# A four-layer graph network on one core: layer 0 of the next group starts on another event, sums and `rf` get two buffers, adj is read twice, one bias add and some copies change engine, and the order of work is found anew

## The chip, the cores and the metric

The kernel runs on one core of one Trainium2 chip. The core has a matrix engine (TensorE, in the profile PE, with its weight loads as PEld), a vector engine (VectorE, DVE), a scalar engine for activations and copies (ScalarE, ACT), a general engine (GpSimd, POOL) and a sync engine (SyncE, SP) from whose queue this kernel issues its DMAs. Each engine takes its instructions in the order of its own queue; engines wait for each other through semaphores.

The metric is the time of one execution on the device in microseconds (us). The median of the runs shown stands for a kernel. About 0.3% is what a measurement of this kernel can tell from no change.

## What is computed

There are 128 graphs of 64 nodes, with 128 features a node (x) and a 64x64 weighted adjacency matrix each (adj). About a quarter of adj is nonzero: an undirected edge is drawn from two chances of 0.125, and the diagonal is always set. The weights are between 0.05 and 5. Four layers follow each other, each as x + layer(relu(layernorm(x))). Cut to what matters:

```python
# layer 0: a filter made from each edge's length, summed over neighbours
g  = exp(coeff * (e[..., None] - offsets)**2)      # e is adj, 64 offsets
h  = ssp(g @ W1.T + b1)                            # ssp(x) = softplus(x) - ln 2
Wf = (h @ W2.T + b2) * A                           # A is adj too
rf = r @ Wa.T                                      # r is the normed x
y  = sum_j rf[j] * (Wf * A)[i, j]
y  = ssp(y @ Wd1.T + bd1) @ Wd2.T + bd2

# layer 1: hyperbolic attention
h = proj(mobius_add(proj(mobius_matvec(W, x)), hyp_bias))
x_loc = logmap(h_i, h_j)                           # for every pair i, j
a = silu(concat(x_self, x_loc) @ att_w1.T + att_b1)
support = sum_j sigmoid(a @ att_w2.T + att_b2) * x_loc * adj
out = proj(expmap(mlp(concat(x_self, support)), h)) # then silu in the tangent space

# layer 2: adj with d_norm on both sides, times x, times W, plus b
# layer 3: concat(x, where(deg > 0, adj.T @ (x @ Ws) / max(deg, 1) + x @ Wr, 0)) @ W_upd
```

Layers 0 and 1 have work for every edge and every feature; they are nearly all of the time. Layers 2 and 3 are small products on whole graphs.

## The kernel before

**Groups and slots.** The graphs are taken in 16 groups of 8. A tile of one group is 128 partitions (two graphs of 64 nodes) by four pairs. The edge work is sparse: in each graph the nodes are sorted by degree, and each node gets a fixed number of slots that its place in this order allows. The slots fall in three classes (c = 0, 1, 2): a graph has 512 slots of class 0 (the first 8 neighbours of each node), 512 of class 1 (the next 8) and 264 of class 2 (what is left, for the 48 nodes of highest degree). `oh` (bf16, 1,288 columns a pair) marks the neighbour that is in a slot, and the weights of the edges, spread over the slots, are the tiles `va`.

**Stages.** Each group goes through seven Python generators, called streams here, of `sparse_stack`:

- `load` (L1384) issues the DMAs of adj (L1389) and x (L1390) on SP's queue.
- `order` (L1395) counts degrees, makes the permutation `perm`, sorts x into `xp` and adj into `adjT` by TensorE products, and makes `oh` by comparing each neighbour's position `pos` with the slot numbers `slot_k`. Within it `normed_x` makes layer 0's `rf`, the tile `a2`.
- `layer0` (L1512) makes the sums over neighbours, `ys` (tiles `y0`, `y1`, `y2`, one for each class). In it `weights_of` makes `va`, the slot weights; `squares` makes the coefficients times weights; `duo` and `filter_of` make the edge filter (`e`, then `ex`, through exp and ln); `neighbours` fetches rf of each slot's neighbour through a TensorE product into PSUM (`big`) and copies it to SBUF as `ra`. VectorE multiplies filter by `ra` (`ex<-big,c_L_gnn_b,ra`) and sums over slots (`y<-ex`).
- `layer1_nodes` (L1652) begins with `bd1` and the softplus of layer 0's output and ends with x after layer 0, `x<-sm,xp`, and the nodes' part of layer 1. Many of its steps are small operations on [128, 4].
- `layer1_edges` is the attention over the same slots: geometric coefficients for each slot (`coefs_of`), a Silu on ScalarE, a Tanh, and weighted sums. `rest1` is the node part behind it, `rest2` (L2121) layers 2 and 3 and the output's DMA (L2239).

**Who sets the order.** The class `Weave` builds the program once, on the host. A stream yields wherever it changes engine, with `on(engine, *takes, after=..., table=...)`: the engine of the next piece, buffers that the piece takes, named events it waits for, and the ScalarE table it needs. `Weave` keeps an estimated clock for each engine and each stream (`about` estimates an instruction). `step` picks, among the pieces that could start soonest on one engine, the one of lowest key; the key is the stream's rank (2 x group + the stage's due) plus an offset from the table `LATE`, which lists one number for each piece of a stream by the stream's name. The queues of PE, DVE, ACT and POOL are then fixed in that order. All instructions but the DMAs are issued in one helper line (L853), so in the profile they are told apart by tile names.

Buffers are counted by `w.ring(n, names)`: n pieces may hold a named buffer at a time, and one that finds it taken can't be picked. The lines that matter here:

```python
w.ring(1, "sm", "sl", "two", "ys", "rf", "U", "a0", "a1", "r0", "x2")
w.ring(2, "va2", "ra", "th", "x", "xp", "nodes", "att", "e")
...
w.ring(5, "adj")
```

So before the change one set of `ys` and one `rf` exist: the layer 0 of two groups cannot be open at once. `layer0(g)` says so too:

```python
yield on(DVE, "ys", after=prior(("order", g), ("layer0", g - 1), ("va1", g - 2)) + [("weights0",)])
```

The event ("layer0", g) comes when all sums of group g are made, ("va0", g) already when its slot weights are made, and ("va1", g) when the weights of the attention of g are.

**The tables of ScalarE.** ScalarE needs a table set loaded for exp and ln, and another for Silu and Tanh. The main loop at the end of `sparse_stack` runs an iteration `it` of four phases, silu, log, silu, log, each with the events that must have come before it ends; with these names the last phase takes layer 0 of group it+2 and the nodes of group it+1, and the third the edges of group `it`. A piece that needs the other table can't be picked.

**adj.** It has five buffers: `order` reads it for the sort, and `rest2`, some three groups later, reads the same tile in its last product.

Of the kernel before, what the change touches and what calls it, by code (L numbers as in the profile page):

```python
# [11 lines left out]
F32 = mybir.dt.float32  # L12
U32 = mybir.dt.uint32
I32 = mybir.dt.int32
# [6 lines left out]
NP = 4  # L21
# [763 lines left out]
def about(engine, op, args, kw):  # L785
# [14 lines left out]
    if engine == ACT:  # L800
# [5 lines left out]


LATE = {
    "attention": (0, -0.5),
    "coefs_of": (1.25, 0.75, -2.25),  # L810
    "coefs_of2": (2.75,),
    "duo": (2.5, 3.5),
    "duo2": (0, 2.5, -2),
    "filter_of": (0.75, 3, -0.25, -2.25, -2, -2.75),
    "filter_of2": (-2.75, 1.75, 2.5, 1.75, -2.5),
    "layer1_nodes": (0, -0.25, 0, 0, 0, 0, 0, 3, -3.5, 0, 0, 0, -0.5, -5.5, 0, 2.25, -1.75, 0, 0, 0,
        0, 0, 0, -2.5, 0, 0, 0, 0, 0, -1.25, 0, 0, 0, 2, 0, 0.75, 0, 0, 0, 0, 0, 0, 0, 0, 0.5),
    "neighbours": (-0.25, -3.5),
    "neighbours2": (1.25,),
    "normed_x": (0, 0, 0, 0, 0, 0, 1.5),  # L820
    "one_minus_z": (3.75,),
    "order": (-0.25, -2.75, 2.25, 0, 0, -5, 0, -3.75, 0, 1.75, -6.75, -3, 3.5, 0, 0, -2.75, -2.75,
        3.25, 1.75, 0.5),
    "rest1": (-3, 0, 0, -3, 0, 0, 0, -3.5, -1.75, 0, 0, 0, 0, 0, -1.75, 0, 0, 0, 3.75),
    "rest2": (2.25, 4.5, 0, 0, 0, 0, 0, 0, 0, 0, 0, -4, 0, -3.75, 0, 1.25, 0, 0, 0, 0, -3, 0, -2.25,
        0, -3.5, 0, 0, 1.25, 3),
    "rows": (0, -1.25),
    "rows2": (2.5,),
    "scores_of": (-1.25, -1.5, -3.5, -1.5),
    "scores_of2": (0, -3.25, 0, -3.5),  # L830
    "slots_ranks": (3.5, 0, 4.75),
    "squares": (2.25, 9.5),
    "squares2": (0, 2.75),
    "turned_from": (3.5,),
    "weights_of": (-3,),
    "weights_of2": (0, -2.5, -2.25),
}


# [30 lines left out]
def on(engine, *takes, after=(), table=None):  # L870

    return engine, takes, after, table
# [98 lines left out]
def sparse_stack(ctx: ExitStack, tc: tile.TileContext, ins, out: bass.AP, flag):  # L971
# [65 lines left out]
    V.tensor_scalar(last_d, bm(ident2, NP), last, None, ALU.mult)  # L1037


    slot_k = const.tile([P, SLOTS + SLOTS % 2], BF, name="slot_k")  # L1040
    slot_r = const.tile([P, SLOTS + SLOTS % 2], BF, name="slot_r")
    rooms = [(name, k) for name in ("e2", "e4", "bR", "rt", "rs", "mask", "e1") for k in range(2)]

    def raw_tile():

# [24 lines left out]
    def slots_ranks():  # L1070
        for c, blocks in enumerate(BLOCKS):
            yield on(DVE)
            at = OFFS[c]
            for k, r0, n, k0 in blocks:
                ki = edge.tile([P, 1024], I32, name="ex", tag="ex", bufs=3)
                G.iota(ki[:, 0:k * n].rearrange("q (n k) -> q n k", n=n), [[0, n], [1, k]], base=k0 - 128,
                       channel_multiplier=0)
                V.tensor_copy(slot_k[:, at:at + k * n], ki[:, 0:k * n])
                V.tensor_copy(slot_r[:, at:at + k * n].rearrange("q (n k) -> q n k", n=n),
                              bl(ident2[:, r0:r0 + n], k))  # L1080
                at += k * n

        w.event("slots")
# [120 lines left out]


    HALF = [slice(0, N), slice(N, P)]
    w.ring(1, "sm", "sl", "two", "ys", "rf", "U", "a0", "a1", "r0", "x2")
    w.ring(2, "va2", "ra", "th", "x", "xp", "nodes", "att", "e")
    w.ring(3, "va", "ex", "big", "oh", "x1")
    w.ring(4, "adjT")  # L1210
    w.ring(5, "adj")

    def evac(dst, src):

# [2 lines left out]
    def wtile(name, bufs=None):  # L1217
        return wide.tile([P, NP, D], F32, name=name, tag=name, **({"bufs": bufs} if bufs else {}))
# [35 lines left out]
    def graphs_mm(pt, lhsT, rhs):  # L1254

        for p in range(NP):
            for h in HALF:
                T.matmul(pt[h, p, :], lhsT=lhsT[h, p, :], rhs=rhs[h, p, :], start=True, stop=True)
# [93 lines left out]
    def part(t, at, k, n):  # L1352

        return t[:, :, at:at + k * n].rearrange("q p (n k) -> q p n k", n=n)
# [28 lines left out]

    def load(g, st):  # L1384
        yield on(DVE, "x", "adj")
        x = st["x"] = pers.tile([P, NP, D], F32, name="x", tag="x")
        adj = st["adj"] = pers.tile([P, NP, N], F32, name="adj", tag="adj", bufs=5)
        gs = slice(2 * NP * g, 2 * NP * (g + 1))
        nc.sync.dma_start(out=adj, in_=adj_d[gs].rearrange("(p b) i j -> (b i) p j", b=2))  # L1389
        nc.sync.dma_start(out=x, in_=x_d[gs].rearrange("(p b) i d -> (b i) p d", b=2))  # L1390
        st["x_used"], st["adj_used"] = w.token("x"), w.token("adj")
        w.wait(5)
        w.event("load", g)

    def order(g, st):  # L1395
# [31 lines left out]
        def normed_x():  # L1427
            yield on(DVE, "a0", "rf")
            st["rf_used"] = w.token("rf")
            raw, mv, sr = ttile("o_raw", NP, 6), ttile("o_mv", NP, 2), ttile("sr", bufs=2)  # L1430
            bn(mv, raw, xp)
            st["sr"] = sr
            yield on(POOL)
            G.tensor_scalar(sr, mv[:, :, 1], EPS_LN, None, ALU.add)
            power(sr, sr, -0.25)
            yield on(POOL)
            h = wtile("a0")
            G.tensor_tensor(h, xp, bl(mv[:, :, 0], D), ALU.subtract)
            yield on(POOL, after=[("weights0",)])
            G.tensor_tensor(xp, xp, bm(bd2s, NP), ALU.add)  # L1440
            yield on(PE, "sm", "a1")
            pt = transposes(h)
            w.release("a0")
            yield on(ACT)
            hT = wtile("a1")
            act(hT, pt, AF.Relu)
            w.release("sm")
            yield on(PE, "sm", after=[("wa",)])
            pt = pairs_mm(hT, lambda p: waT)
            w.release("a1")  # L1450
            yield on(ACT)
            st["rf"] = wtile("a2")
            evac(st["rf"], pt)
            w.release("sm")
            w.event("rf", g)
# [2 lines left out]
        yield on(PE, "sm")  # L1458
        pt = bank(N)
        graphs_mm(pt, adj, perm)  # L1460
        yield on(ACT)
        half = etile("o0")
        evac(half, pt[:, 0:NP, :])
# [19 lines left out]
        for c in range(3):  # L1483
            for at, k, r0, n in blocks_of(c):
                yield on(DVE, after=[("slots",)])
                at += OFFS[c]
                ks = slot_k[:, at:at + k * n].rearrange("q (n k) -> q n k", n=n)
                V.tensor_tensor(part(oh, at, k, n), bl(pos[:, :, r0:r0 + n], k),
                                ks.unsqueeze(1).to_broadcast([P, NP, n, k]), ALU.is_equal)
        yield on(DVE, after=[("rf", g)])  # L1490
        w.event("order", g)

# [18 lines left out]

    def layer0(g, st):  # L1512

        yield on(DVE, "ys", after=prior(("order", g), ("layer0", g - 1), ("va1", g - 2)) + [("weights0",)])
        oh, adjT, rf, sr = st["oh"], st["adjT"], st["rf"], st["sr"]
        ys = st["ys"] = [wtile(f"y{c}") for c in range(2)]
        ys.append(wide.tile([P, 2 * NP, RC], F32, name="y2", tag="y2"))
        st["ys_used"] = w.token("ys")
        ras = {}

# [31 lines left out]
        def neighbours(c, p, k, factors):  # L1552

            yield on(PE, "big", "ra", after=[("f", g, c, p)])
            W = WIDTHS[c]
            nb = big()
            for b, rows in enumerate(HALF):
                T.matmul(nb[:, b, 0:W], lhsT=rf[rows, p, :], rhs=factors[0][rows, k, :],
                         start=True, stop=True)
            factors[1]()  # L1560
            w.event("nb", g, c, p)
            yield on(ACT)
            ra = edge.tile([P, 2, 512], F32, name="ra", tag="ra")
            act(ra[:, :, 0:W], nb[:, :, 0:W], AF.Copy)
            w.release("big")
            ras[c, p] = ra, w.token("ra")
            w.event("ra", g, c, p)
# [86 lines left out]
    def layer1_nodes(g, st):  # L1654
# [9 lines left out]
        T.matmul(pre.rearrange("q (x r) -> q x r", r=N)[:, :, 0:RC], lhsT=wd1T, rhs=ys[2],  # L1664
                 start=False, stop=True)
        w.release("ys", st["ys_used"])
        yield on(DVE)
        V.tensor_scalar(flat(spn), pre, bd1, None, ALU.add)
        w.release("sm")
        V.tensor_scalar(ex, spn, SOFT_MAX, None, ALU.min)  # L1670
        w.event("soft_ready", g)
        yield on(ACT, table="log")
# [181 lines left out]
        V.scalar_tensor_tensor(e1, gram, -2.0, h2b, ALU.mult, ALU.add)  # L1854
        V.tensor_tensor(e3, e1, R, ALU.add)
        V.scalar_tensor_tensor(e3, e3, 0.0, e2, ALU.max, ALU.mult)
        rt, rs, mask = etile("rt"), etile("rs"), etile("mask")
        V.tensor_scalar(rt, e3, MIN_NORM2, None, ALU.max)
        yield on(ACT, table="log")
        act(rt, rt, AF.Ln)  # L1860
# [20 lines left out]
        V.scalar_tensor_tensor(rt, e4, -0.5, rt, ALU.mult, ALU.add)  # L1881
        V.tensor_tensor(rt, rt, rs, ALU.mult)
        yield on(DVE)
        series(rt, e3, mask, rs)
        yield on(DVE)
        V.tensor_tensor(rt, rt, e2, ALU.mult)
        qd = dense.tile([P, NP, 2, N], F32, name="qd", tag="qd", bufs=2)
# [232 lines left out]

    def rest2(g, st):  # L2121

        yield on(PE, "sm", after=prior(("rest1", g), ("rest2", g - 1)) + [("weights2",)])
        adj, adjT, x2 = (st[n] for n in ("adj", "adjT", "x2"))
        gs = slice(2 * NP * g, 2 * NP * (g + 1))
        dn = ttile("dn")
        pt = bank()
        for p in range(NP):
# [103 lines left out]
        yield on(PE, "sm")  # L2232
        pt = bank()
        graphs_mm(pt, adj, xs)
        w.release("adj", st["adj_used"])
        yield on(DVE)
        plus_scaled(y, pt, rdeg, y)
        w.release("sm")
# [64 lines left out]
```

## Time and profile before

| what | us |
|---|---|
| runs, median (lowest to highest) | 2124.67 (2119.98 to 2125.86) |
| the profiled execution, its own time | 2121.52 |
| its span, first to last instruction | 2119.6 |
| PE busy (11,223 instructions) | 1806.3 (85%) |
| PEld busy | 866.0 (41%) |
| DVE busy (4,828) | 1847.9 (87%) |
| ACT busy (3,364) | 1641.1 (77%) |
| POOL busy (362) | 364.5 (17%) |
| chain that ended last, by engine | PE 37%, DVE 36%, ACT 19%, issue 7% |
| DMA, all queues | 13.94 MB, 7 GB/s mean |

Busy is the time in which an engine had an instruction at work; several engines are busy at once, so the shares don't add up. The chain is followed back from the last instruction to whatever released each step, and its shares do. DMA is of no weight: the 16 DMA engines are at work for a few per cent of the span. The page's slices show how even the run is between its start and its end:

```profile
PE   4869897998989898998989889898989889896773
PEld 2333343444444344444444444444434444443342
DVE  5669789999999999999999999999999999897742
ACT  3767887979698887979798897969888796975531
```

Each digit is the busy share, in tenths (9 is 90% or more), of one of 40 slices of 53 us. Three of the costlier groups of instructions give a feeling for the sizes:

```profile
L853 PE MATMUL big<-ex,w2T 128*128 128x512 f32 (+1 forms) x768 | 320.2, 542 | 41.8 <-ACT ex L853 20.6
L853 ACT ACTIVATE ra<-big 128x528 f32<-128x528 f32 (+1 forms) x192 | 166.3, 886 | 8.1 <-PE big L853 7.6
L853 DVE SCALAR_TENSOR_TENSOR ex<-big,c_L_gnn_b,ra 128x1024 f32<-128x1024 f32 x128 | 163.7, 1279 | 16.0 <-PE big L853 15.6
```

A row has the line, the engine, the operation, the tile written and those read, the size and the number of instructions; then their busy time in us and the mean of one in ns; then the engine's idle time just before them and what ended most of it.

### The profile page before, as it was taken

The numbers are of one execution on the slowest core, as the hardware profiler recorded it, in microseconds if no ns is written. First come the engines' busy times: TensorE is split into PE (matmuls) and PEld (weight loads), VectorE is DVE, ScalarE is ACT, GpSimd is POOL, SyncE is SP. The second block draws the span as 40 slices with busy tenths as digits, with TensorE's granted clock in tenths as the row PEclk, the third lists the DMA queues.
The fourth block names the chain that finished last, engine by engine and source line by source line (L and its number), as shares of the span: only waits on it lengthen the run. The fifth ranks groups of instructions, "written<-read, shape, count | busy, mean of one in ns | idle before, by whom it ended". The sixth has DMA issues, their size and how long they took to land.

```text
span 2119.6 us, 31941 instructions
## 1 busy us (share of the span) xinstructions
PE 1806.3 (85%) x11223; PEld 866.0 (41%) x11223; DVE 1847.9 (87%) x4828; ACT 1641.1 (77%) x3364; POOL 364.5 (17%) x362
## 2 busy tenths in 40 slices
PE   4869897998989898998989889898989889896773
PEld 2333343444444344444444444444434444443342
DVE  5669789999999999999999999999999999897742
ACT  3767887979698887979798897969888796975531
POOL 1011012021212203021221202121220302111121
PEclk9979999999999999999999999999999999997765
DMA  2000000000000000000000000000000000000000
GB/s 55 3 6 1 1 6 1 6 8 6 1 8 6 8 6 8 6 8 6 1 8 6 9 6 9 6 1 8 6 9 1 9 1 6 1 1 6 6 5 8
DMA packets 29531, 13.94 MB, mean 7 GB/s; under 512 B 10544, under 2 KB 29360, under 8 KB 29360
## 3 DMA queue, kind: packets, MB, share of 16 engines
q1 hardware_dynamic: 29360, 11.80, 2.1%
q8 instruction: 90, 1.47, 0.3%
q14 instruction: 81, 0.66, 0.1%
HBM read 7.61 MB, written 4.19 MB: 6 GB/s over the span
## 4 chain that ended last, share of the span: by engine, by line
PE 37%; DVE 36%; ACT 19%; issue 7%; POOL 0%; SPq 0%; DMA 0%; DVEq 0%; ACTq 0%; POOLq 0%
PE big L853 25%; PE sm L853 9%; ACT ex L853 6%; DVE va L853 5%; DVE ex L853 4%; PE sl L853 4%; ACT e L853 4%; DVE th L853 4%; DVE y L853 2%; ACT ra L853 2%; DVE ah L853 2%; DVE v L853 2%; ACT n L853 2%; DVE att L853 2%; DVE oh L853 1%
## 5 line engine op out<-in xcount | busy, mean ns | idle before, releaser
L853 PE MATMUL big<-ex,w2T 128*128 128x512 f32 (+1 forms) x768 | 320.2, 542 | 41.8 <-ACT ex L853 20.6
L853 ACT ACTIVATE ex<-big,c_L_gnn_att_b 128x1024 f32<-128x1024 f32 (+1 forms) x192 | 185.5, 974 | 105.0 <-PE big L853 103.2
L853 PE MATMUL big<-e,w1T 64*128 64x512 f32 (+1 forms) x768 | 201.5, 624 | 68.0 <-ACT e L853 47.8
L853 ACT ACTIVATE ex<-big,c_L_gnn_b 128x1024 f32<-128x1024 f32 (+1 forms) x192 | 185.7, 976 | 44.1 <-PE big L853 44.0
L853 PEld LDWEIGHTS big<-ex,w2T 128*128 128x128 f32 x768 | 131.7, 189 | 198.6 <-ACT ex L853 69.5
L853 PE MATMUL big<-va,U 64*128 64x512 f32 (+1 forms) x768 | 186.5, 563 | 29.1 <-DVE va L853 26.8
L853 PE MATMUL big<-va,a 64*128 64x512 f32 (+1 forms) x768 | 181.1, 568 | 10.7 <-DVE k_s L853 3.8
L853 PE MATMUL sl<-ex,aw2b 128*64 128x512 f32 (+1 forms) x768 | 180.7, 549 | 5.5 <-ACT th L853 4.3
L853 DVE SCALAR_TENSOR_TENSOR ex<-big,c_L_gnn_b,ra 128x1024 f32<-128x1024 f32 x128 | 163.7, 1279 | 16.0 <-PE big L853 15.6
L853 ACT ACTIVATE ex<-ex 128x1024 f32<-128x1024 f32 (+1 forms) x192 | 173.9, 925 | 0.2
L853 ACT ACTIVATE ra<-big 128x528 f32<-128x528 f32 (+1 forms) x192 | 166.3, 886 | 8.1 <-PE big L853 7.6
L853 DVE TENSOR_REDUCE y<-ex 128x128 f32<-128x1024 f32 x128 | 155.3, 1213 | 0.6
L853 ACT ACTIVATE th<-sl,hab 128x512 f32<-128x512 f32 (+1 forms) x192 | 118.1, 615 | 45.4 <-PE sl L853 45.4
L853 PE MATMUL big<-slot_r,Sx 64*128 64x512 bf16 (+1 forms) x1152 | 138.9, 346 | 0.0
L853 POOL TENSOR_TENSOR k_r<-k_r,exp 128x4 f32<-128x4 f32 x32 | 32.4, 1013 | 583.1 <-DVE k_r L853 578.7
L853 PEld LDWEIGHTS big<-e,w1T 64*128 64x128 f32 x768 | 68.9, 204 | 155.6 <-ACT e L853 55.1
L853 ACT ACTIVATE va<-va,sr 128x512 f32<-128x512 f32 (+1 forms) x192 | 123.1, 650 | 3.1 <-DVE va L853 2.9
L853 PE MATMUL big<-oh,pqs 64*64 64x512 bf16 (+1 forms) x1152 | 123.3, 348 | 0.0
L853 DVE COPY_PREDICATED va<-slot_r,big 128x1024 f32<-128x1024 uint16 (+1 forms) x96 | 106.5, 1111 | 9.7 <-PE big L853 9.7
L853 DVE SCALAR_TENSOR_TENSOR th<-th,oh 128x1024 f32<-128x1024 f32 (+1 forms) x80 | 99.2, 1240 | 13.8 <-ACT th L853 13.8
L853 ACT ACTIVATE e<-e 128x1024 f32<-128x1024 f32 (+2 forms) x144 | 106.7, 752 | 1.1
L853 PE MATMUL big<-va,ones 64*64 64x512 f32 (+1 forms) x768 | 97.4, 559 | 11.0 <-DVE va L853 11.0
(479 smaller groups left out, 3832.4 us busy)
## 6 DMA issues: line engine op xcount, KB each, us to landing
x<-in_x_dram SPq DMA_DIRECT2D x16, 256.0 KB, 2.9
out_dram<-v SPq DMA_DIRECT2D x16, 256.0 KB, 2.3
adj<-in_adj_dram SPq DMA_DIRECT2D x16, 128.0 KB, 2.3
rt<-in_L_gnn_att_w_dram SPq DMA_DIRECT2D x2, 64.0 KB, 1.9
rs<-in_L_gnn_mlp_w_dram SPq DMA_DIRECT2D x2, 64.0 KB, 2.0
wupd<-in_L_gnn_W_upd_dram SPq DMA_DIRECT2D x1, 128.0 KB, 3.6
w<-in_L_gnn_W_msg_dram SPq DMA_DIRECT2D x2, 64.0 KB, 3.3
r_L_gnn_bd<-in_L_gnn_bd_dram SPq DMA_DIRECT2D x1, 64.0 KB, 3.1
```

The lines of the kernel that those rows point to most:

```text
L853: return f(*args, **kw)
```

## The change

1. `layer0(g)` begins after ("va0", g-1), when the group before has its slot weights, in place of ("layer0", g-1), when it has its sums. `ys` and `rf` have two buffers each.
2. `x` and `adj` have one buffer in place of two and five. `order` gives adj back after its product, and `rest2` reads adj again from DRAM, into a tile of its own, `adj2`, with one buffer.
3. `bd1` is added on ScalarE (Identity with a bias), and VectorE's clamp of it is a piece of its own that waits for that.
4. The copy of `ra` from PSUM is on VectorE for groups 0 and 1, and on ScalarE as a plain copy for the others.
5. `slot_k` loses the slots of class 1, whose numbers are those of class 0 plus 8; the comparison for class 1 subtracts the 8 from `pos` in the same instruction. The tile `mask` in `series` is replaced by `e4`, which is free there.
6. The table `LATE` is new, for every stream.

```diff
 LATE = {
-    "attention": (0, -0.5),
-    "coefs_of": (1.25, 0.75, -2.25),
...
+    "attention": (3, 2.5),
+    "coefs_of": (-3.5, -0.25),
...
-    slot_k = const.tile([P, SLOTS + SLOTS % 2], BF, name="slot_k")
+    slot_k = const.tile([P, SLOTS - OFFS[1]], BF, name="slot_k")
...
-    w.ring(1, "sm", "sl", "two", "ys", "rf", "U", "a0", "a1", "r0", "x2")
-    w.ring(2, "va2", "ra", "th", "x", "xp", "nodes", "att", "e")
+    w.ring(1, "sm", "sl", "two", "x", "adj", "adj2", "U", "a0", "a1", "r0", "x2")
+    w.ring(2, "va2", "ra", "th", "ys", "rf", "xp", "nodes", "att", "e")
     w.ring(3, "va", "ex", "big", "oh", "x1")
     w.ring(4, "adjT")
-    w.ring(5, "adj")
...
-            st["rf"] = wtile("a2")
+            st["rf"] = wtile("a2", 2)
...
         graphs_mm(pt, adj, perm)
+        w.release("adj", st["adj_used"])
...
-                V.tensor_tensor(part(oh, at, k, n), bl(pos[:, :, r0:r0 + n], k),
-                                ks.unsqueeze(1).to_broadcast([P, NP, n, k]), ALU.is_equal)
+                if c == 1:
+                    V.scalar_tensor_tensor(part(oh, at, k, n), bl(pos[:, :, r0:r0 + n], k), -8.0, ks,
+                                           ALU.add, ALU.is_equal)
+                else:
+                    V.tensor_tensor(part(oh, at, k, n), bl(pos[:, :, r0:r0 + n], k), ks, ALU.is_equal)
...
-        yield on(DVE, "ys", after=prior(("order", g), ("layer0", g - 1), ("va1", g - 2)) + [("weights0",)])
+        yield on(DVE, "ys", after=prior(("order", g), ("va0", g - 1), ("va1", g - 2)) + [("weights0",)])
...
-            yield on(ACT)
+            first = g < 2
+            yield on(DVE if first else ACT)
             ra = edge.tile([P, 2, 512], F32, name="ra", tag="ra")
-            act(ra[:, :, 0:W], nb[:, :, 0:W], AF.Copy)
+            (V.tensor_copy if first else S.copy)(ra[:, :, 0:W], nb[:, :, 0:W])
...
-        yield on(DVE)
-        V.tensor_scalar(flat(spn), pre, bd1, None, ALU.add)
-        w.release("sm")
+        yield on(ACT)
+        act(flat(spn), pre, AF.Identity, bias=bd1)
+        w.release("sm")
+        yield on(DVE)
         V.tensor_scalar(ex, spn, SOFT_MAX, None, ALU.min)
...
-        yield on(PE, "sm", after=prior(("rest1", g), ("rest2", g - 1)) + [("weights2",)])
-        adj, adjT, x2 = (st[n] for n in ("adj", "adjT", "x2"))
+        yield on(DVE, "adj2", after=prior(("edges", g), ("rest2", g - 1)))
+        adj, adj_used = pers.tile([P, NP, N], F32, name="adj2", tag="adj2", bufs=1), w.token("adj2")
         gs = slice(2 * NP * g, 2 * NP * (g + 1))
+        nc.sync.dma_start(out=adj, in_=adj_d[gs].rearrange("(p b) i j -> (b i) p j", b=2))
+        w.wait(5)
+        yield on(PE, "sm", after=prior(("rest1", g)) + [("weights2",)])
+        adjT, x2 = (st[n] for n in ("adjT", "x2"))
...
-        w.release("adj", st["adj_used"])
+        w.release("adj2", adj_used)
```

## The prediction

> **What bounds the kernel now.** The page's busy times come first: VectorE (DVE) 1847.9 of the span's 2119.6 us, TensorE (PE) 1806.3, ScalarE (ACT) 1641.1. VectorE leads, but that is an average over start, middle and end. I cut the span at a landmark that each group has once, VectorE's addition `x<-sm,xp`, called x1(g) here: it stands a few us behind the end of group g's layer 0. The view of the tile x dates the first and last; the timeline has x1(2) at 342.2 and x1(14) at 1801.6. The view of windows then gives for each stretch its length, PE, PEld, DVE, ACT and POOL busy, the granted clock:
>
> ```profile
> L853 DVE TENSOR_TENSOR x<-sm,xp x16: 679/686/697, 106.5 to 1902.2; 128x512 f32<-128x512 f32 x16
> ```
> ```profile
> 39.20:106.50 67.30, 55.37 (x260) 23.51 (x260) 44.42 (x71) 51.79 (x68) 0.00 (x0) 0.97 0.02 5
> 106.50:342.20 235.70, 198.44 (x1089) 85.96 (x1089) 195.31 (x454) 180.04 (x343) 31.12 (x27) 0.93 0.01 3
> 342.20:1801.60 1459.40, 1309.67 (x8396) 623.24 (x8394) 1376.86 (x3583) 1228.05 (x2521) 275.31 (x253) 0.98 0.02 6
> 1801.60:1902.20 100.60, 88.49 (x519) 41.13 (x521) 89.08 (x236) 88.86 (x183) 14.12 (x14) 0.97 0.00 1
> 1902.20:2119.60 217.40, 139.42 (x889) 83.02 (x889) 122.51 (x417) 88.05 (x242) 35.13 (x40) 0.67 0.02 6
> ```
>
> The reader is to see three regimes. In the middle, twelve groups of 121.6 us, VectorE is busy 1376.9/1459.4 = 94.3%: that is VectorE's bound, and what is left is small gaps between instructions. From x1(0) to x1(2) it is busy only 195.3/235.7 = 82.9%, with no engine above 85%: there the order of the work is the limit. After x1(15) it is busy 56%: one group's chain runs out. The timeline of VectorE shows what the start waits for:
>
> ```profile
> 96.46 1.21 DVE L853 TENSOR_REDUCE y<-ex 128x128 f32<-128x1024 f32 x1
> ...
> 117.07 0.17 DVE L853 TENSOR_SCALAR nn<-n 128x8 f32<-128x8 f32 x1 [5.89 <-ACT n L853]
> ...
> 125.96 4.62 DVE L853 TENSOR_TENSOR va<-oh,adjT 128x1024 f32<-128x1024 bf16 x4
> ```
>
> Group 0's last sum is made at 96.5, and group 1's first slot weights (`va<-oh,adjT`) only at 126.0, with VectorE idle in between.
>
> Inside one group of the middle there are two halves, divided by ScalarE's table loads. The first row is the half with the exp/ln table, the second the longest part of the half with the silu table:
>
> ```profile
> 722.10:784.30 62.20, 54.24 (x329) 25.89 (x329) 57.45 (x168) 58.29 (x110) 7.82 (x8) 0.97 0.02 5
> 784.30:822.70 38.40, 35.41 (x198) 15.87 (x199) 37.17 (x87) 24.53 (x61) 11.20 (x9) 1.00 0.00 1
> ```
>
> In the first ScalarE is the fuller (58.3/62.2 = 94%), in the second VectorE (97%). The middle is thus a VectorE bound with ScalarE close behind in one half.
>
> **The change, part by part.** The built programs give each engine's instructions in order, without times. I walked VectorE's in both and priced each by what its kind adds to VectorE's busy time before. These are queue sums, not times.
>
> | VectorE's queue sum, us | before | after |
> |---|---|---|
> | to x1(0) | 61.7 | 79.8 |
> | group 1's slot weights | 74.2 to 88.7 | 71.8 to 79.6 |
> | x1(0) to x1(2) | 196.5 | 188.8 |
> | x1(2) to x1(14) | 1378.3 | 1368.7 |
> | x1(14) to x1(15) | 89.1 | 113.1 |
> | x1(15) to the end | 122.3 | 112.0 |
> | all | 1847.9 | 1862.5 |
>
> *The earlier layer 0, two buffers for its sums and for rf.* Group 1's weights now stand ahead of x1(0). But from group 2 on they do not: group 2's weights stand at 171.1 behind x1(1) at 169.4, and in the middle group g+1's stand 13 us behind x1(g), where before they began 2 us ahead of it. There another wait rules: layer 0 of g also waits for the coefficients of g-2, and these for the weights of g-1. So the new condition is worth something at the start alone.
>
> *ra of groups 0 and 1 on VectorE.* 16 copies of 1024 and 8 of 528 columns out of PSUM. No such row exists; nearest is the three-operand pass over the same PSUM tile, 1279 and 762 ns, as the upper end. The lower end is half of it, if a copy ran two columns a cycle; but VectorE's pass out of PSUM takes 746 ns for 512 columns (row below) where the one out of SBUF, `a<-a`, takes 426, so I take 1.25 and 0.75: 16 x 1.25 + 8 x 0.75 = 26 us more on VectorE, 16 x 0.95 + 8 x 0.57 = 20 less on ScalarE. Half of it falls before x1(0), where VectorE idles 22.9 of 67.3 us and ScalarE is the fuller: covered.
>
> *bd1 on ScalarE, slots of class 1.* The rows, of four groups of the middle, then one of ScalarE over the middle:
>
> ```profile
> L853 DVE TENSOR_SCALAR a<-sm,c_L_gnn_bd 128x512 f32<-128x512 f32 x4 | 3.0, 746 | 1.5 <-PE sm L853 1.5
> L853 DVE TENSOR_TENSOR oh<-pos,slot_k 128x2048 bf16<-128x2048 bf16 x8 | 18.1, 2257 | 0.0
> L853 DVE SCALAR_TENSOR_TENSOR th<-th,oh 128x1024 f32<-128x1024 f32 x16 | 19.4, 1210 | 0.0
> L853 DVE TENSOR_TENSOR va<-oh,qd 128x1024 f32<-128x1024 bf16 x16 | 19.1, 1215 | 0.0
> ```
> ```profile
> L853 ACT COPY a<-sm x24: 577/582/587, 429.6 to 1790.8; 128x512 f32<-128x512 f32 x24
> ```
>
> bd1 takes 0.75 us from VectorE (0.68 net of overlap) and puts some 0.6 on ScalarE, per group: 12 x 0.68 = 8 us in the middle. A rule speaks against it: the Trainium skill, "ScalarE: Activation LUTs", Rules for kernel authors, wants additions on VectorE. By the rule these 8 us stay; by the rows (746 against 582 ns, and the fuller queue is VectorE's) the move pays. I go by the rows. It adds a wait: VectorE's clamp behind it now needs ScalarE. In VectorE's queue the clamp stands behind `th<-th,oh`, which needs the Tanh just ahead of the bias add on ScalarE; that pass lasts 1.2 us, the add 0.6. So I take 0. If the add came late by one Silu and one Tanh (1.7 us), the waiting reductions `att<-th` and slots behind it would lose 12 x 1.7 = 20.
>
> The slots of class 1 become a pass with a scalar (-8) in place of a plain comparison. "VectorE: DVE Perf Modes", The perf-mode tier table, gives `tensor_tensor` in bf16 two columns a cycle (1224 ns at 2048), and lists nothing of the kind for the form with a scalar: by it the change would cost up to 1.03 us a group, 12 in the middle. But the row takes 2257 ns for these 2048 columns, one a cycle, and the two forms cost the same over 1024 (1210, 1215). I take 0; the ends are -1 and 12.
>
> *adj read twice, single buffers.* 16 more loads of 128 KB, 2.3 us to landing in the page's DMA list, 0.37 us of SP's queue each. adj and x of g+1 now wait for TensorE's products in order(g): one group early in the middle; at the start adj(0) is free at 29.4, its load lands by 33, and order(1) began at 43.7. The second adj waits on SP ahead of the group's output, both on the same group's last product, so it holds nothing back. The dropped mask changes no count; slot_k's missing class saves 0.4 us at the start.
>
> **The sum.** x1(0): from 39.2 VectorE has 79.8 - 17.7 = 62 us, at 94.3% 66 us: 105 (before 106.5). x1(0) to x1(2): at best 188.8/0.943 = 200; with the edges' chain of group 0 still in it I take 92%: 205, so x1(2) at 310, 32 earlier. Middle: 1368.7/0.943 = 1451, 8 less. Then the new order has more ahead of x1(15): 113.1/0.943 = 120, 19 more; behind it 10 us less VectorE work, of which I give the chain 8: 209. 310 + 1451 + 120 + 209 = **2090**, 30 under the span. The profiled execution took 2121.5, 1.9 above its span: 2092; the runs' median is 3.2 above that execution: **2095**, 1.4% faster.
>
> **Rivals.**
> *ScalarE's half becomes the period (slower).* With the exp/ln table, ScalarE's queue holds 60.9 us a group in the new order, 58.5 before (rf's two copies and one more ra moved in). It is 94% full there, so that half grows 2.4/0.94 = 2.6 us. If the other half, 97% full of VectorE work, gives none back, a group takes +2.6 where I have -0.7: 12 x 3.3 = 40, 2135. Against it: VectorE's sum per group falls, so work that fits in the longer half leaves the other. It decides from 2.5 us a group.
> *The start stays a chain.* x1(0) to x1(2) at the old 82.9%: 228, 23 lost: 2118. For it: group 1's edges still wait for group 0's nodes, whose small operations idle VectorE. Against: that idle time is what group 1's layer 0 now fills.
> *All of it.* 200 in the start, and x1(14) to the end as before (318): 16 more: 2079. Against: the 24 us moved ahead of x1(15) are in the queue.
>
> **Chances.** Forecast 0.50, ScalarE's half 0.18, start a chain 0.20, all of it 0.12. No change is within 0.3% (6 us), about what this measurement can tell. Faster takes the first and last, and most of the third: 0.75; same 0.08; slower 0.17. The range reaches to both outer cases: 2074 to 2133; the forecast's own is 2082 to 2112.
>
> **What would show it.** Right: group 1's weights at 85 to 92 before x1(0), x1(2) at 305 to 318, the middle 120 to 121.6 a group with VectorE at 94%, x1(14) to x1(15) near 120. Wrong: a middle above 123 with ScalarE waits ahead of VectorE's `ex` passes or clamps, or x1(2) after 325.

## The result, and the profile after

The changed kernel takes 2173.49 us (median of 4 runs, 2170.09 to 2174.5) against 2125.27 in the runs beside it: a ratio of 1.0229, 95% interval 1.0208 to 1.025. It is 48 us **slower**; 2095 was predicted, 1.4% faster. The profiled execution has a span of 2170.1 us, 80 over the predicted 2090.

These are the rows of the view of windows, cut at the same landmarks as before the change (from group 0's slot weights to x1(0), x1(2), x1(14), x1(15) and the end). Columns: window, length, then busy us of PE, PEld, DVE, ACT, POOL, then TensorE's granted clock, DMA share and GB/s.

```profile
40.00:112.70 72.70, 62.02 (x291) 26.81 (x291) 62.29 (x102) 50.15 (x66) 3.57 (x4) 0.97 0.02 6
112.70:334.30 221.60, 187.30 (x1008) 81.18 (x1008) 186.36 (x398) 157.82 (x296) 18.61 (x19) 0.93 0.02 4
334.30:1835.20 1500.90, 1326.72 (x8350) 633.53 (x8350) 1389.48 (x3575) 1228.31 (x2527) 260.17 (x252) 0.96 0.03 7
1835.20:1965.00 129.80, 113.78 (x695) 54.64 (x693) 114.00 (x309) 107.21 (x234) 19.13 (x19) 0.95 0.03 7
1965.00:2170.10 205.10, 130.36 (x809) 78.42 (x809) 114.78 (x384) 81.62 (x229) 34.91 (x38) 0.66 0.02 6
```

The start brings 8 us (x1(2) at 334.3, before 342.2), not 32, although group 1's slot weights do come early, as VectorE's timeline shows (126.0 before):

```profile
103.39 3.49 DVE L852 TENSOR_TENSOR va<-oh,adjT 128x1024 f32<-128x1024 bf16 x3
...
112.66 0.69 DVE L852 TENSOR_TENSOR x<-sm,xp 128x512 f32<-128x512 f32 x1
```

The twelve middle groups take 125.1 us each, before 121.6: 41 us lost. From x1(14) to the end it is 334.9 us, before 318.0: 17 lost. In the middle VectorE is busy for 12.6 us more than before, although its queue holds less work, and yet for a smaller share (1389.5/1500.9 = 92.6%, before 94.3%); TensorE is busy for 17 us more with no more products (8350, before 8396), at a lower clock. So two things happened in the middle: VectorE's instructions got longer, and it waits.

Where, the same view shows inside one group. The half with the exp/ln table took 62.2 us before; here it takes 71.9 (734.6 to 806.5), and this is it in three pieces:

```profile
734.60:752.00 17.40, 12.50 (x60) 5.15 (x60) 14.82 (x68) 14.61 (x23) 4.57 (x5) 0.80 0.09 24
752.00:764.00 12.00, 8.82 (x38) 3.89 (x40) 10.03 (x23) 8.24 (x22) 1.26 (x1) 0.72 0.00 0
764.00:806.50 42.50, 40.50 (x267) 21.04 (x267) 38.47 (x86) 38.11 (x71) 5.27 (x5) 1.00 0.04 10
```

No engine is full in the first 29 us, and TensorE's clock is 0.80 and then 0.72 of full speed; behind that it is 1.00. Before, the clock fell once in a group, in the first 16 us of this half (0.89 there), and was 1.00 for the other 46.

The timelines show where. First TensorE in the changed kernel: start, duration, instruction, and in brackets its idle time before and what ended that.

```profile
737.04 5.49 PE L852 MATMUL big<-e,w1T 64*128 64x512 f32 x12 [2.83 <-ACT e L852]
...
747.09 1.88 PE L852 MATMUL big<-ex,w2T 128*128 128x512 f32 x4
...
755.91 3.78 PE L852 MATMUL big<-ex,w2T 128*128 128x512 f32 x4 [3.18 <-DVE ex L852]
```

The wait of 2.83 us at 737 is for the first Exp behind the table load; the kernel before has one of 3.05 at the same place. The second, 3.18 us, is new: TensorE wants a PSUM buffer `big` that VectorE's multiplication `ex<-big,c_L_gnn_b,ra` has to give back. Then four products of the same shape last 3.78 us in place of 1.88, twice as long, and VectorE in turn waits for them (1.70 below). The Trainium skill, "TensorE: Matmul & The Clock Gate", Part 1, says that the array runs at half clock after a window of too little work until it has been busy for one; 3.78 against 1.88 is that factor, and the granted clock is 0.50 from 753.2 to 760.0 us, with 1.00 on either side. It fell half a us into the 3.18 us wait, so this wait alone did not bring the fall; TensorE had stood idle for 1.10 us shortly before.

And this is VectorE just there, in the changed kernel:

```profile
748.39 0.75 DVE L852 TENSOR_SCALAR th<-th 128x4 f32<-128x4 f32 x1
749.05 0.15 DVE L852 TENSOR_SCALAR at_k<-arg 128x4 f32<-128x4 f32 x1
749.24 1.24 DVE L852 COPY_PREDICATED th<-at_k,th 128x4 f32<-128x4 uint32 x1
...
752.34 1.25 DVE L852 TENSOR_SCALAR cc<-xx 128x4 f32<-128x4 f32 x1
...
754.58 1.28 DVE L852 SCALAR_TENSOR_TENSOR ex<-big,c_L_gnn_b,ra 128x1024 f32<-128x1024 f32 x1
...
759.73 1.28 DVE L852 SCALAR_TENSOR_TENSOR ex<-big,c_L_gnn_b,ra 128x1024 f32<-128x1024 f32 x1 [1.70 <-PE big L852]
```

and in the kernel before:

```profile
734.46 0.17 DVE L853 COPY_PREDICATED th<-at_k,th 128x4 f32<-128x4 uint32 x1
734.54 1.28 DVE L853 SCALAR_TENSOR_TENSOR ex<-big,c_L_gnn_b,ra 128x1024 f32<-128x1024 f32 x1
735.73 0.71 DVE L853 TENSOR_SCALAR th<-th 128x4 f32<-128x4 f32 x1
```

Before, the multiplication stands right behind `th<-at_k,th`, 12.4 us after the table load. In the new order eighteen instructions stand between the two, and it comes 19.9 us after the load. Fifteen of them are the rest of the nodes' chain, on 128x4; the other three stood ahead of it before as well. The second thing to see is that three of these small instructions last 0.75, 1.24 and 1.25 us, where such a one takes 0.16. GpSimd's timeline has, at these moments:

```profile
748.07 1.03 POOL L852 TENSOR_TENSOR w<-hh,cs 128x512 f32<-128x512 f32 x1
749.19 1.27 POOL L852 TENSOR_TENSOR w<-w,r_L_gnn_mlp_b 128x512 f32<-128x512 f32 x1
752.31 1.26 POOL L852 TENSOR_TENSOR x<-x,r_L_gnn_b 128x512 f32<-128x512 f32 x1 [1.85 <-ACT v L852]
```

Each long one starts with, or inside, an operation of GpSimd over 128x512, and ends with it. Held against the usual duration of its kind, a group of the middle has 6.1 us of such stretching in seven instructions; the kernel before had 4.5 in five. One of the five is easily missed, since it is stretched in every group of the middle (in the changed kernel the same instruction takes 357 ns):

```profile
L853 DVE TENSOR_TENSOR att<-att,att 128x192 f32<-128x192 f32 x12 | 14.8, 1232 | 0.4
```

The expectation for the kernel before in the last experiment was written without it: it speaks of 3.5 us in four. Over twelve groups the difference is 19 us; VectorE's busy time grew by 12.6, so what it had to do was lighter, by some 7 us where the queue sums have 10.

### The profile page after: what moved, and what is told of

Read it like the earlier page. It is cut to its first block, busy times and chain, and to the rows that moved or that the text cites. A ratio compares the mean times of both kernels' runs of the same rounds, so it can differ in the third digit from the quotient of the medians.

```text
span 2170.1 us, 31945 instructions
## 1 busy us (share of the span) xinstructions
PE 1835.0 (85%) x11223; PEld 883.8 (41%) x11223; DVE 1886.4 (87%) x4835; ACT 1629.4 (75%) x3356; POOL 344.0 (16%) x361
## 4 chain that ended last, share of the span: by engine, by line
DVE 47%; PE 32%; ACT 16%; issue 4%; POOL 0%; DMA 0%; SPq 0%; DVEq 0%; ACTq 0%; POOLq 0%
PE big L852 22%; PE sm L852 8%; DVE th L852 4%; ACT ex L852 4%; DVE va L852 4%; DVE ex L852 4%; DVE e L852 4%; DVE oh L852 4%; DVE y L852 3%; DVE att L852 3%; DVE ah L852 2%; ACT e L852 2%; ACT n L852 2%; ACT w L852 2%; PE sl L852 2%
## 5 line engine op out<-in xcount | busy, mean ns | idle before, releaser
L852 PE MATMUL big<-ex,w2T 128*128 128x512 f32 (+1 forms) x768 | 348.8, 580 | 61.0 <-DVE ex L852 46.0
L852 PEld LDWEIGHTS big<-ex,w2T 128*128 128x128 f32 x768 | 139.9, 201 | 202.2 <-issue 86.7
L852 ACT COPY ra<-big 128x1024 f32<-128x1024 f32 (+1 forms) x168 | 145.5, 878 | 48.0 <-PE big L852 48.0
L852 PEld LDWEIGHTS big<-e,w1T 64*128 64x128 f32 x768 | 73.9, 214 | 152.4 <-ACT e L852 54.8
L852 ACT ACTIVATE va<-va,sr 128x512 f32<-128x512 f32 (+1 forms) x192 | 121.2, 657 | 13.8 <-DVE va L852 13.5
L852 POOL TENSOR_TENSOR k_r<-k_r,exp 128x4 f32<-128x4 f32 x32 | 41.4, 1295 | 514.6 <-DVE k_r L852 514.6
L852 DVE TENSOR_TENSOR va<-oh,adjT 128x1024 f32<-128x1024 bf16 (+6 forms) x160 | 118.3, 780 | 2.4 <-PE big L852 1.8
```

Of the source, the lines that this page charges most:

```text
L852: return f(*args, **kw)
```

## The experiments

In the first four runs the planner chose the order from the table `LATE`. In all later ones the order is held: the pieces of the streams are issued from a list recorded from one of the two kernels, so that an edit moves no other piece. Which of the three `big` buffers a product gets is not in the list, and in one run that changed too (see the last experiment). The edit is the same in all:

```diff
     def step(self):
-        ready = [(t, s.key, k) for k, s in enumerate(self.streams) if (t := self.begin(s)) is not None]
...
+        k = next(self.plan, None)
+        if k is None:
+            return False
+        t = self.begin(self.streams[k])
+        assert t is not None
+        s = self.streams[k]
         self.now, s.t = s, t
```

Theory A was that the new order is at fault, theory B that the pieces of the change are, in any order.

### Order against pieces

Four kernels: each structure with the other's table (a 0 put in for the two new pieces, or their numbers left out), and each with an empty one.

```diff
 LATE = {
-    "attention": (3, 2.5),
...
+    'attention': (0, -0.5),
...
```

> All of the change but its new offsets: the table of offsets is the old one, with a 0 put in for each of the two new pieces. Theory A (the found order is at fault: it puts the small node operations ahead of layer 0's multiplications, TensorE runs dry and its clock falls): the second dip of the clock in the exp/ln half goes, a group takes about 122 us, and the time is between 2095 and 2135. Theory B (the pieces of the change cost it, whatever the order: bd1's new wait, the copies on VectorE, the single buffers, the earlier layer 0): still about 2170, a group near 125.

> The kernel before with the new offsets alone (those of the two new pieces left out). Theory A: slower than before by about what the change lost, 2150 to 2185, with TensorE dry for 3 us in the exp/ln half of each group. Theory B: within 10 us of 2125.

> The whole change with no offsets at all (the table is empty), to be set beside the kernel before with none. Theory A: the same as or up to 30 us faster than that one, since the earlier layer 0 then only fills the start. Theory B: slower than that one by 30 to 60 us.

> The kernel before with no offsets at all. Both theories: slower than 2125, since the offsets were found for it; by 20 to 80 us. It is the base for the run beside it.

| | its own table | the other's | none |
|---|---|---|---|
| kernel before | 2124.5 | 2352.7 | 2410.3 |
| changed kernel | 2173.5 | 2193.8 | 2415.1 |

With no offsets the two structures differ by 5 us: theory B's 30 to 60 are not there. But A's numbers were missed as well: the old table does not make the changed kernel fast (2194, a group 128.2 us), and the new one makes the old structure much slower than I had. A table of offsets belongs to the structure that it was found for; it is worth 286 us to the kernel before, where I had expected 20 to 80, and 242 to the changed one. So these runs say that the order decides, but not what is wrong in it.

### One instruction a group

The list of the changed kernel, with the pieces of the nodes of group g, of layer 0 of g+1 and of the rest of g-1 that stand at this place:

```diff
+    filter_of(c=0, p=0) #4      DVE  ex<-big,c_L_gnn_b,ra
     layer1_nodes #21            DVE  th, xy, xx, ca, den, cc: fifteen on 128x4
     rest1 #2                    DVE  r<-sm,ident and qd<-qd,r
-    filter_of(c=0, p=0) #4      DVE  ex<-big,c_L_gnn_b,ra
```

> The changed kernel in its own order, with one VectorE instruction moved in each group from 1 on: layer 0's first multiplication, which gives TensorE a PSUM buffer back, stands ahead of the second half of the nodes' small operations (some 20 instructions on 128x4) in place of behind them. Theory A (the found order starves TensorE there, and the lower clock after it makes VectorE wait): TensorE's wait of 3.2 us ahead of that group's second filter product falls below 1.5, the second dip of the clock goes, a group takes 122 to 123.5 us in place of 125.1, and the time is 2130 to 2155. Theory C (VectorE has simply more to do, since more of its instructions collide with GpSimd's, and the waits on TensorE only show where it would be late anyway): a group stays at 124.5 to 125.5, the time within 8 us of 2173.

2138.36 us, ratio to the kernel before 1.008 (1.0061 to 1.0099): 35 of the 48 us are back, with one VectorE instruction moved in each of fourteen groups, and a group takes 122.5 us. The middle in the view of windows:

```profile
334.80:1805.20 1470.40, 1314.57 (x8350) 628.43 (x8350) 1387.18 (x3575) 1227.06 (x2527) 260.07 (x252) 0.97 0.03 7
```

VectorE is busy for nearly as long as in the changed kernel (1387.2, there 1389.5), but its share is back at 94.3% (1387.2/1470.4), as before the change. TensorE's timeline in this run, the same group:

```profile
738.50 2.79 PE L909 MATMUL big<-ex,w2T 128*128 128x512 f32 x4
...
744.05 1.98 PE L909 MATMUL big<-ex,w2T 128*128 128x512 f32 x4
```

The second row is the product that had waited for 3.18 us and taken 3.78: it waits for nothing and takes 1.98. (The one before it takes 2.79 here and 1.88 there, so a little of the low clock is left.) Theory C, that the waits are only where VectorE would be late anyway, falls.

The run beside it moves one thing more, layer 2's degree product on TensorE (`sm<-ones,adjT`), ahead of the three filter products that it stood behind:

> The same, and TensorE's small product of layer 2's degrees (ones x adjT) stands ahead of layer 0's first three filter products in place of behind them, so that VectorE's dn does not wait for them. Theory A: VectorE's 1.3 us wait at dn goes too: 0.5 to 1.5 us a group less than the run beside it, 6 to 18 us in all. Theory C: no difference between the two.

2131.32 us, ratio 1.0026 (1.0008 to 1.0043), a group 122.2: 7 us less in the medians, at the low end of A's range, but this kernel's runs lie far apart (2121 to 2137) and a group is only 0.35 us shorter.

### The pieces, one at a time, in a held order

bd1 alone, in the kernel before and its order:

```diff
-        yield on(DVE)
-        V.tensor_scalar(flat(spn), pre, bd1, None, ALU.add)
+        yield on(ACT)
+        act(flat(spn), pre, AF.Identity, bias=bd1)
         w.release("sm")
+        yield on(DVE)
```

> The kernel before in its own order, with bd1 alone moved to ScalarE, at its place in ScalarE's queue. My prediction: 0.7 us a group less on VectorE, 5 to 10 us faster. Theory B (the parts themselves cost time): slower by 5 to 20 us, since VectorE's clamp waits behind ScalarE's Silu and Tanh. Theory A: between 2115 and 2128, no more than that.

2122.53 us, ratio 1.0001 (0.9992 to 1.001): nothing. VectorE is busy for 8.4 us less over the middle (1368.5, before 1376.9), as I had it, but the clamp behind the add waits. Its row over four groups, idle time and its cause last:

```profile
L910 DVE TENSOR_SCALAR a<-a 128x512 f32<-128x512 f32 x4 | 1.7, 427 | 3.4 <-ACT a L910 3.4
```

3.4/4 = 0.85 us a group, in place of the 0.7 saved.

The copies of ra, in the changed kernel and its order:

```diff
-            yield on(DVE if first else ACT)
+            yield on(ACT)
...
-            (V.tensor_copy if first else S.copy)(ra[:, :, 0:W], nb[:, :, 0:W])
+            S.copy(ra[:, :, 0:W], nb[:, :, 0:W])
```

> The changed kernel in its own order, with the ra copies of groups 0 and 1 back on ScalarE. My prediction: VectorE had room for them at the start and ScalarE had not, so the start gets 0 to 15 us longer, the middle the same: 2173 to 2188. Theory B: the copies cost VectorE 26 us there, so 5 to 20 us faster, 2153 to 2168.

2173.93 us, x1(2) at 335.4 (334.3 with the copies on VectorE): the 24 copies don't matter on either engine.

The condition and the second set of sums, there too:

```diff
-    w.ring(1, "sm", "sl", "two", "x", "adj", "adj2", "U", "a0", "a1", "r0", "x2")
-    w.ring(2, "va2", "ra", "th", "ys", "rf", "xp", "nodes", "att", "e")
+    w.ring(1, "ys", "sm", "sl", "two", "x", "adj", "adj2", "U", "a0", "a1", "r0", "x2")
+    w.ring(2, "va2", "ra", "th", "rf", "xp", "nodes", "att", "e")
...
-        yield on(DVE, "ys", after=prior(("order", g), ("va0", g - 1), ("va1", g - 2)) + [("weights0",)])
+        yield on(DVE, "ys", after=prior(("order", g), ("layer0", g - 1), ("va1", g - 2)) + [("weights0",)])
-        ys = st["ys"] = [wtile(f"y{c}", 2) for c in range(2)]
+        ys = st["ys"] = [wtile(f"y{c}") for c in range(2)]
...
```

> The changed kernel in its own order, with the old condition for layer 0 (the group before has all its sums) and one buffer for the sums in place of two; rf keeps its two. In the order of the changed kernel, layer 0 of a group is begun behind the end of the one before, and behind the read of its sums, in all sixteen groups, so every engine's queue stays the same, instruction for instruction. Theory D (the new condition and the second set of sums bring nothing and cost nothing in this order): within 5 us of 2173, start and middle alike. My prediction's step, that the condition is what brings the start forward: the start gets some 20 us longer.

2172.73 us, x1(2) at 330.1, a group 125.1. The part of the change that it is named for, the new condition with a second set of sums, is not used: in the order that was found, every group's layer 0 is begun behind the end of the one before. What is used is rf's second buffer, which the next two kernels take away, for group 1 and for all:

```diff
         def normed_x():
-            yield on(DVE, "a0", "rf")
+            yield on(DVE, "a0", "rf", after=[("layer0", 0)] if g == 1 else [])
```

> The changed kernel in its own order, but rf of group 1 (its layer norm, transposes and product, nine pieces) waits for the end of group 0's layer 0, as it had to when rf had one buffer; every other group as it was. Theory F (rf's second buffer, not the condition, brings group 1's slot weights forward, from 126 to 103 us, and that is worth the 8 us by which x1(2) comes earlier than before): group 1's weights back near 120 or later, x1(2) 5 to 15 us later than 334, the middle at 125.1, so 2178 to 2190. Theory G (the start is bound by group 0's edges whatever stands ahead): x1(2) within 4 us of 334, the time within 5 of 2173.

> The same for all groups: rf has one buffer, and its pieces come as soon behind the end of the layer 0 before as that allows, every other piece in the changed kernel's order. Theory F: the start as in the run beside it. In the middle rf is needed only at the next layer 0, some 90 pieces later, so a group takes 124 to 127 us: 2170 to 2210. If rf's place in the middle were what starves TensorE: a group under 123.5.

With rf of group 1 late, 2178.75 us: x1(2) comes at 345.3, 11 us later, and the middle stays at 125.2. So theory F holds in the time: the 8 us at the start come from rf. It fails in the way it gave for them. Group 1's slot weights hardly move: three of the first four still come from 104.7 on (103.4 with the early rf), and the last at 119.9. What comes 12 us later is x1(0), at 125.1, behind rf's pieces, which now begin at 103.2 and not at 54.0. With one buffer in all groups (each rf piece as early as that allows) 2285.08 us and 132.3 a group, more than the 124 to 127 expected: the order leans on the early rf in every group. It is not what starves TensorE.

### GpSimd's operations on VectorE

Theory E was that an operation of GpSimd over 128x512 holds a VectorE instruction up for longer than VectorE would need to do it itself. Five a group are moved, at their place:

```diff
-            yield on(POOL)
+            yield on(DVE)
             h = wtile("a0")
-            G.tensor_tensor(h, xp, bl(mv[:, :, 0], D), ALU.subtract)
+            V.tensor_tensor(h, xp, bl(mv[:, :, 0], D), ALU.subtract)
...
-            G.tensor_tensor(u, hh, bl(st["cs"], D), ALU.mult)
-            G.tensor_tensor(u, u, bm(mb2, NP), ALU.add)
+            for p in range(NP):
+                V.scalar_tensor_tensor(u[:, p, :], hh[:, p, :], st["cs"][:, p:p + 1], mb2, ALU.mult, ALU.add)
```

(likewise `xp` + bd2, the product of `mx` with the bias, and `x2` + b).

> The changed kernel in its own order, with five additions and multiplications over 128x512 a group moved from GpSimd to VectorE, at their place (layer 0's h and bd2, the product with the bias, x_self as four fused passes, layer 2's bias). Theory E (each of these stalls one VectorE instruction by 0.6 to 1.1 us while it runs, 5 us a group in all, more than the 3.9 us that VectorE needs to do them itself, and three of them stall the small operations ahead of layer 0's first multiplication): 1 to 3 us a group less, 2120 to 2160. If the long VectorE instructions are no stall by GpSimd: 3.9 us more VectorE work a group, 2200 to 2235.

> Both moves of the run after_ex_dn (layer 0's first multiplication and layer 2's degree product earlier), and these five operations on VectorE. Theory E: 1 to 1.7 us a group under after_ex_dn's 122.2, so 2105 to 2120, faster than the kernel before. Otherwise: 2170 to 2195.

> The kernel before in its own order with the same five operations on VectorE. It loses 3.5 us a group to four such stalls, and VectorE would need 3.9 for the five operations. Theory E: within 10 us of 2123. If the long instructions are no stall by GpSimd: 2165 to 2190.

| | us | ratio to before (interval) | a group |
|---|---|---|---|
| changed kernel, five operations moved | 2113.46 | 0.9957 (0.9943 to 0.9972) | 120.6 |
| the same, with the two moves of after_ex_dn | 2099.30 | 0.9889 (0.9873 to 0.9906) | 119.6 |
| kernel before, five operations moved | 2114.41 | 0.9959 (0.9945 to 0.9973) | 121.4 |

The middle of the second, in the view of windows:

```profile
336.00:1771.10 1435.10, 1291.57 (x8348) 618.36 (x8348) 1360.10 (x3670) 1223.77 (x2527) 172.37 (x180) 0.99 0.03 7
```

VectorE has five operations a group more and is busy for 1360.1 us, 29 less than in the changed kernel as it was (1389.5). Of 6.1 us stretching a group 0.6 is left, at `k_s`, beside a GpSimd operation that was not moved. The granted clock is 0.99. The clean comparison is this kernel with after_ex_dn: 2131.32 to 2099.30 us, 2.6 us a group, where theory E had 1 to 1.7. The kernel before gains 7.5 us in all: there the move ended 4.5 us of stretching a group, for an estimated 3.9 us of new work on VectorE.

The changed kernel alone gains 60 us, 4.4 a group, but not from the stalls alone. The product that had waited 3.18 us for `ex` no longer waits for it; in this run it starts ahead of `ex`, which begins at 737.51:

```profile
737.26 1.98 PE L909 MATMUL big<-ex,w2T 128*128 128x512 f32 x4 [0.46 <-ACT ra L909]
```

The product behind it, `big<-va,a`, waits for `ex` in its place, in every group of the middle. It looks as if the two had exchanged `big` buffers, though no piece was moved; why stays open. So a part of the 60 us is a cure of the same wait that the order's two moves end, and the cures overlap: 2.9 us a group by the order, 4.4 by the operations, 5.5 by both. The kernel of the second row is 1.1% faster than the kernel before, and beats both.

## Why the prediction was wrong

Against the predicted span of 2090, 80 us are to be accounted for: 24 at the start, 50 in the middle, 10 between x1(14) and x1(15), 4 less behind that.

**What bounds the kernel.** The three regimes were read rightly. The step from them, that the middle runs at VectorE's queue sum divided by 94.3%, was the error that cost most: I took that share for a property of the engine, and it was one of the order. Of the 50 us in the middle, 22 are VectorE's longer instructions ((1389.5 - 1368.7)/0.943), and the other 28 the fall of the share to 92.6%, that is the waits for TensorE. They stand nearly all at one instruction, here over the twelve groups before and after, with its idle time last:

```profile
L853 DVE SCALAR_TENSOR_TENSOR ex<-big,c_L_gnn_b,ra 128x1024 f32<-128x1024 f32 x96 | 122.7, 1278 | 3.0 <-PE big L853 2.6
L852 DVE SCALAR_TENSOR_TENSOR ex<-big,c_L_gnn_b,ra 128x1024 f32<-128x1024 f32 x96 | 122.5, 1276 | 43.3 <-PE big L852 43.3
```

With one instruction a group moved, the share is 94.3% again. I had priced an instruction by what its kind took before, and the small ones of 1.0 to 1.2 us that the trace of before already held (`s<-nn`, 1234 ns for 128x4, in the same view as my rows) I had counted as a cost of their kind in place of asking what they waited for.

**The earlier layer 0.** "The new condition is worth something at the start alone" was wrong: it is worth nothing anywhere, since no group uses it. I had seen group 1's weights move ahead of x1(0) in the built order, and had put it down to the condition without asking which event or buffer it had waited for before. They do come early (103.4, 9 us ahead of x1(0)), but neither the condition nor, for three of the first four, rf's second buffer is what brings them; what does stays open. The size was off as well: 8 us in place of 32. To x1(0) VectorE is busy 62.3 of 72.7 us, 86%, where I had taken 94.3%: 8 of the 24 us lost. From x1(0) to x1(2) VectorE is busy 186.4/221.6 = 84%, where I had taken 92%: rival two's mechanism, a start that stays a chain, which had said 83%. Its emptiest part is the silu half of group 0's edges (189.2 to 239.2), 50 us with VectorE busy for 36.7 and a longest wait of 3.6 us for a Tanh on ScalarE; x1(1) and some slot weights of group 2 stand there, but do not fill it.

**ra on VectorE.** The sizes were right (1216 and 698 ns, taken as 1250 and 750), and "covered" was right.

**bd1 on ScalarE.** ScalarE takes 687 ns for it, against 0.6 us taken, and VectorE's 8 us are saved. "I take 0" for the new wait failed in the old order, where it is 0.85 us a group; in the changed kernel's own order none shows at the clamp in the middle, and three in the whole run (1.3, 1.3 and 0.8 us). It is worth nothing where I measured it.

**Slots of class 1.** The rows of four groups bear out the 0, with the scalar and without; by itself this part was not tried.

```profile
L852 DVE TENSOR_TENSOR oh<-pos,slot_k 128x2048 bf16<-128x2048 bf16 x4 | 9.2, 2292 | 0.0
L852 DVE SCALAR_TENSOR_TENSOR oh<-pos,slot_k 128x2048 bf16<-128x2048 bf16 x4 | 9.0, 2260 | 0.0
```

**adj read twice.** Right: one wait of 1.0 us for an adj DMA in the whole run.

**The end.** 129.8 + 205.1 = 334.9, where I had 120 + 209 = 329. That the new order has more ahead of x1(15) was right, and it is a lasting cost: in the fastest kernel here the tail still takes 326.1 us, before 318.0, where layer 0's weights now begin 13.8 us behind x1 of the group before and not 2.3 ahead of it, so that the last group's layer 0 begins later. That this is the cause was not tried.

**The rivals.** 2135 for "ScalarE's half becomes the period" had the right half and the right sign of it, for a wrong reason: in that half ScalarE is busy for 61.0 of 71.9 us, 85%, so it isn't the bound. Its 2.6 us a group resemble the 3.5 measured by accident. That the order itself could be the worse one was no rival of mine, though it is by far the largest part of the change. My range ended at 2133, short even of that rival's own 2135.

## What to carry to other kernels

When a change brings a new order, a queue sum is not enough: go through the built order at the places where one engine gives a buffer back to another, and ask what has come to stand ahead of the instruction that does it. Ask of each added buffer or condition whether the order that was built uses it at all; here one of the two second buffers was in use in every group, and the other, like the condition, in none. And before work is sent to GpSimd to spare VectorE, look at VectorE's instructions at these moments: an operation that VectorE does in 0.69 us cost it up to 1.1 us when GpSimd did it. Last, when one of two kernels with the same order is faster, see whether each wait still ends at the same instruction: a list of pieces does not hold the buffers.

## What the hardware showed that I had not expected

In the changed kernel each of the seven GpSimd operations over 128x512 in a group holds up one VectorE instruction, most of them until they end, be this a copy, a pass with a scalar or one with two operands, down to 128x4: 0.16 us becomes 1.25 (`cc<-xx` above), 0.33 becomes 1.42 (a `va<-oh,adjT`). Not every instruction is held: a reciprocal on 128x4 at 748.18, in the midst of `w<-hh,cs`, took its usual 0.18. And GpSimd can be the one that waits: in the kernel before, `a<-xp,o_mv` and `xp<-xp,r_L_gnn_bd`, which take 1.14 and 1.34 us in the changed kernel, took 2.52 and 3.34 beside two comparisons for `oh` (2.26 and 2.25 us) that had begun first. The Trainium skill, "SBUF — State Buffer", SBUF: two separate sides, describes an exclusive lock on a port pair that the two engines share, held for the whole instruction by whichever came first; the starts and ends in the timelines agree with that. GpSimd's powers on 128x4, which take 1.0 to 1.1 us each, held nothing up: at 746.0 and 746.4, beside `k_r<-k_r,exp`, two VectorE passes over 128x256 took their usual 0.42. Both inputs of these passes are in SBUF, so by the section they would have had to wait; here the page and the trace differ.

TensorE's clock made the miss larger than the waits alone: in the group shown the 3.18 us wait was followed by four products at twice their time, and over the whole run the products with w2T averaged 580 ns, before 542.
